# The last rows of a mixture of experts: one-hot products in PSUM in the place of a scatter and a load

## The chip, the core and the metric

The program runs on one core of a Trainium2 chip. The metric is the device time of one execution in microseconds (us). An execution under the profiler is read beside it; its times are counted from the first instruction of the span. The engines are TensorE (PE, with its weight loads as PEld), VectorE (DVE), ScalarE (ACT), GpSimd (POOL) and SyncE (SP, which issues DMAs).

## What is computed

Layer 0 is a non-local convolution block. Layer 1 takes its 2 x 3136 tokens of 256 channels through causal attention and a mixture of eight experts, of which each token uses two:

```python
t = t + attention(ln(t))
xf = ln(t).reshape(-1, 256)
probs = softmax(xf @ gate_w + gate_b)
top2_vals, top2_idx = top_k(probs, 2)
for e in range(8):            # 256 -> 512 -> 256
    y = gelu(xf @ W1[e] + b1[e]) @ W2[e] + b2[e]
    out += cw[:, e, None] * y # cw is 0 but for the two chosen
t = t + out
```

The result is handed back with the channels first, so each tile of 128 tokens has to be transposed at the end.

## The kernel before

**Stages.** Layer 0 and the first projections take about 110 us. Attention runs from there to about 860 us, batch 0 and then batch 1. In the same time each token's two rows (one for each chosen expert) get a place ("slot") in a list sorted by expert, and the normalized rows are scattered into it (`x_slots`, L1302 for both batches). The list has 105 blocks of 128 rows, and a block belongs to one expert. Blocks 0 to 41 hold rows of batch 0 alone, 42 to 56 rows of both, and the later ones rows of batch 1. The first 102 blocks are worked through by `experts` (`MAIN = NBLK - GB = 102`); if the rows need more blocks, or the sums of the softmax are out of bounds, a branch at the end of the program (`tc.If`, L1977) does the rest or does all again. With these inputs it is not entered, so it is a jump to the end. What it compares is `good`, computed by `judge` (L1632, L1633) and loaded into every engine's registers by `count` (L1971) after everything else.

**The expert stage.** From 864 to 1276 us the loop in `experts` takes one block n per step. The order of instructions is written out by hand (`manual_schedule`):

- `fetch` loads a group of three blocks' rows (SP, L1342), `load` works out where the results go (DVE, three small operations, L1367 to L1372: the row number in `y_tokens`).
- `hidden(n)`: 8 products of 128 x 128 x 128 (L1421) and four Gelus on ACT (L1430). In fp32, PE takes each product in two passes, so the profile counts 16.
- `inputs(n + 2)`: two transposes (L1398) and a copy by ACT (L1402).
- `weights(n + 2)`: a copy of the expert's first weights by DVE (L1409).
- `outputs(n - 3)` (`LATE = 3`): 4 products with the expert's second weights (L1440, 8 passes of 256 columns), then the sum with the bias on DVE (L1450, two halves). The block's 128 rows `ys` go, for n below 57, to `y_slots` in slot order, and for n from 42 on POOL scatters them to `y_tokens` in token order (L1457).
- `between()` gives the two `finish` generators a turn, and `experts_of` loads expert numbers into the registers of PE and DVE (L1384).

So second products run three blocks behind first products, and after block 101's first product four second products (98 to 101) are left.

**The finish.** From block 57 on `written` starts `finish(0)` and `finish(1)`. A piece is a pair of tiles of 128 tokens: two sets of rows, one for each of a token's two experts, are brought into SBUF. For batch 0 POOL gathers them from `y_slots` (L1514). For batch 1, whose rows are in token order, SP loads them from `y_tokens` (L1539) once the blocks that can hold them have been scattered (`complete(n)`: the list is sorted, and within an expert by token). DVE adds both, times the gate's weights, to the token's own row (L1554). PE transposes into a bank of PSUM (L1567), ACT copies it out (L1572) and SP stores it (L1573). The tiles `ot` have two buffers, the `y` tiles of batch 1 three. Batch 1's tiles 20 to 24 need block 101 or one close to it, so these pieces come after the last second product. A tile's rows can be loaded only when the scatters that it waits for have landed in DRAM. SP's queue works in order: a store that waits holds up what stands behind it.

Of the kernel before, what the change touches and what calls it, by code (L numbers as in the profile page):

```python
# [10 lines left out]
F32 = mybir.dt.float32  # L11
# [17 lines left out]
def conv_attn_moe_kernel(  # L29
# [74 lines left out]
    XS = C + 2  # L104
# [9 lines left out]
    MAIN = NBLK - GB  # L114
    SCALE = 1.0 / HS**0.5
    LEAST, MOST = 1e-25, 1e25
    assert B == 2 and NBLK % GB == 0 and FULL0 % GB == 0 and QB % (2 * P) == 0 and NS == NB and all(e >= min(N, (i + 1) * W) for i, (_, e) in enumerate(SEGS))
# [318 lines left out]
    wts = [const.tile([P, NCH, 2], F32, name=f"wt{b}") for b in range(B)]  # L436
# [12 lines left out]
    def layer1(nm, general):  # L449

        with ExitStack() as whole:
# [491 lines left out]
            def dispatch(b):  # L943
# [345 lines left out]
                for n in range(NCH):  # L1289
# [9 lines left out]
                    if b:  # L1299
                        nc.vector.tensor_copy(xr[:kk, C:], t[:kk, n, TOKEN : SLOT + 1])  # L1300
# [18 lines left out]
            def experts(w1s, w2s, b2s, ex, es, ps6, between, need, written):  # L1319
# [40 lines left out]
                def load(g, xb, other):  # L1360
# [3 lines left out]
                    if b:  # L1364
# [3 lines left out]
                            eq, xb[:, :, C + 1], sid[:, s - FULL0 : e - FULL0], ALU.is_equal  # L1368
                        )
                        nc.vector.tensor_scalar(eq, eq, -float(N), float(N + OFF), ALU.mult, ALU.add)  # L1370
                        to = ex.tile([P, GB], U32, tag="to", bufs=4, name=f"to_{nm}_{g}")
                        nc.vector.tensor_tensor(to, eq, xb[:, :, C], ALU.add)  # L1372
# [62 lines left out]
                def outputs(n, state):  # L1435
# [20 lines left out]
                    if n >= FULL0:  # L1456
                        s = nc.gpsimd.indirect_dma_start(  # L1457
# [16 lines left out]

                fetched, groups, ids, xin, wb, act = [], [], [], {}, {}, {}
                for n in range(-1, MAIN + LATE):
# [14 lines left out]
                    if 0 <= n - LATE < MAIN:  # L1491
                        outputs(n - LATE, act.pop(n - LATE))
# [5 lines left out]
            def finish(b, oy, bufs):  # L1498
# [27 lines left out]
                def complete(n):  # L1526


                    return min(MAIN, (2 * N + 2 * n * P) // P + E)

# [29 lines left out]
                def store(n, m, k, ys, rows):  # L1560
# [12 lines left out]
                    nc.sync.dma_start(  # L1573
# [5 lines left out]
                parts = deque(pairs())  # L1579
                while b == 0 and (parts or ahead):  # L1580
# [14 lines left out]
                while parts or ahead or added:  # L1595
                    now = worked[0]
                    over = now == MAIN
                    if parts and len(ahead) + bool(added) < bufs:
                        n, m, k = parts[0]
                        of = complete(n + m)  # L1600
                        if over or now >= min(of + GAP, max(of, MAIN - 1)):
                            ahead.append((now, load(*parts.popleft())))
                            yield True
                            continue
                    if added and (over or now > added[0]):
                        store(*added[1])
                        added = None
                        yield True
                    elif ahead and not added and (over or now >= ahead[0][0] + GAP):
# [431 lines left out]
```

## Time and profile before

| | us |
|---|---|
| median of 3 runs | 1336.9 (1336.3 to 1340.93) |
| the profiled execution's own time | 1298.01 |
| its span | 1296.3 |
| PE busy | 1251.2 (97%) |
| DVE, ACT, POOL busy | 792.1, 611.2, 351.1 |
| last second product ends | 1276.0 |
| last scatter issued | 1277.3 |
| last store issued | 1288.0 |

The page of a profile gives busy time by engine and then the span in 40 slices, one digit for each (9 is 90% busy or more); a slice is 32.4 us here. `PEclk` is the clock that TensorE was granted, in tenths. The chain is the work that ended last, followed backwards: at each step to what released it. In its listing by time a row has start, length and what ran. A row of a line has the engine, the operation, the tiles written and read, shape and count.

### The profile page before, as it was taken

How to read it: one execution, taken by the hardware profiler on the slowest of the kernel's cores; microseconds unless marked ns; L12 is line 12 of the kernel's file. 1: busy time of each engine (PE TensorE's matmuls, PEld its weight loads, DVE VectorE, ACT ScalarE, POOL GpSimd, SP SyncE). 2: the span in 40 equal slices, each digit the busy share in tenths (PEclk: the TensorE clock that was granted, in tenths of full speed). 3: DMA queues.
4: the chain of work that ended last, by engine and by line, in shares of the span. 5: the costliest groups of instructions: out<-in, count | busy, mean ns of one | idle time of the engine just before them, and what ended most of it. 6: DMA issues, size and time to landing. Idle time of an engine off the chain costs nothing.

```text
span 1296.3 us, 28049 instructions
## 1 busy us (share of the span) xinstructions
PE 1251.2 (97%) x10569; PEld 821.7 (63%) x10569; DVE 792.1 (61%) x1659; ACT 611.2 (47%) x1228; POOL 351.1 (27%) x317
## 2 busy tenths in 40 slices
PE   8998999999999999999999999999999999999994
PEld 7874445444444454534444444469899899999993
DVE  1582557676777764668687877755675443465553
ACT  0144555565656555356555655552433333444441
POOL 1102412110002204221115760000047312675641
PEclk9999999999999999999999999999999999999997
DMA  9994011000000000100001243231135443576553
GB/s 304 384 310 165 16 25 32 25 9 25 9 17 9 26 1 12 38 9 16 9 9 62 93 158 108 60 111 50 58 123 171 128 114 95 148 234 200 183 162 104
DMA packets 110656, 123.55 MB, mean 95 GB/s; under 512 B 20020, under 2 KB 100261, under 8 KB 110513
## 3 DMA queue, kind: packets, MB, share of 16 engines
q1 hardware_dynamic: 97104, 93.12, 23.7%
q0 software_dynamic: 9984, 25.76, 5.9%
q10 hardware_dynamic: 3424, 2.78, 0.7%
q8 instruction: 87, 1.43, 0.5%
q14 instruction: 57, 0.46, 0.1%
HBM read 62.65 MB, written 60.41 MB: 95 GB/s over the span
## 4 chain that ended last, share of the span: by engine, by line
PE 80%; DVE 6%; issue 5%; DMA 3%; ACT 2%; POOL 2%; POOLq 0%; DVEq 0%; ACTq 0%; SPq 0%
PE yp_f L700 17%; PE sc_f L660 16%; PE ht_f L1421 13%; PE yp_f L1440 12%; PE qk_f L540 6%; PE cp L330 3%; PE v_f L557 3%; DVE acc_f L682 3%; PE gram L261 3%; PE pp_f L610 2%; POOL x_slots L1302 2%; ACT st_f L668 2%; PE tp_f L1398 2%; DMA kept<-t 1%; PE sp_f L724 1%
## 5 line engine op out<-in xcount | busy, mean ns | idle before, releaser
L668 ACT ACTIVATE st_f<-sc_f 128x896 f32<-128x896 f32 (+5 forms) x400 | 331.0, 840 | 214.7 <-PE sc_f L660 197.3
L682 DVE TENSOR_TENSOR acc_f<-acc_f,st_f 128x896 f32<-128x896 f32 (+5 forms) x372 | 379.6, 1020 | 67.3 <-ACT st_f L668 55.8
L700 PE MATMUL yp_f<-st_f,v_f 64*64 64x448 f32 (+6 forms) x3184 | 339.8, 501 | 4.3 <-DVE st_f L670 3.0
L660 PE MATMUL sc_f<-qT_f,kT_f 64*64 64x448 f32 (+6 forms) x3184 | 339.7, 499 | 3.3 <-ACT st_f L668 2.1
L1430 ACT ACTIVATE g_f<-ht_f,b1b 128x128 f32<-128x128 f32 x408 | 116.7, 369 | 222.5 <-PE ht_f L1421 222.5
L660 PEld LDWEIGHTS sc_f<-qT_f,kT_f 64*64 64x64 f32 x3184 | 122.4, 133 | 154.4 <-issue 124.7
L700 PEld LDWEIGHTS yp_f<-st_f,v_f 64*64 64x64 f32 x3184 | 119.8, 133 | 155.3 <-issue 131.1
L1421 PE MATMUL ht_f<-xT_f,w_f 128*128 128x128 f32 x1632 | 200.3, 276 | 0.8 <-ACT xT_f L1402 0.8
L1421 PEld LDWEIGHTS ht_f<-xT_f,w_f 128*128 128x128 f32 x1632 | 197.1, 193 | 5.7 <-ACT xT_f L1402 1.0
L712 POOL TENSOR_TENSOR qT_f<-both_f 128x448 f32<-128x448 f32 x28 | 37.0, 1322 | 488.5 <-ACT both_f L711 488.5
L1302 POOL DMA_INDIRECT x_slots<-xr_f,idx x100 | 111.2, 1112 | 127.4 <-DVE xr_f L1300 90.0
L511 POOL TENSOR_SCALAR xn_f<-t 128x256 f32<-128x256 f32 (+1 forms) x50 | 80.3, 1614 | 170.9 <-PE xp_f L526 66.2
L1409 DVE COPY w_f<-w1s_f 128x1024 f32 x102 | 71.6, 704 | 55.3 <-PE ht_f L1421 53.6
L1457 POOL DMA_INDIRECT y_tokens<-ys_f,to_f x60 | 62.4, 1040 | 120.6 <-DVE ys_f L1450 95.2
L1450 DVE TENSOR_TENSOR ys_f<-yp_f,kT_f 128x128 f32<-128x128 f32 x102 | 29.6, 290 | 100.7 <-PE yp_f L1440 96.5
L540 PE MATMUL qk_f<-px_f,wat 128*128 128x512 f32 (+2 forms) x224 | 88.1, 546 | 1.2 <-ACT px_f L532 1.2
L540 PEld LDWEIGHTS qk_f<-px_f,wat 128*128 128x128 f32 x224 | 40.6, 190 | 46.9 <-issue 41.6
L670 DVE TENSOR_TENSOR st_f<-st_f,keep 128x256 f32<-128x256 f32 (+1 forms) x112 | 45.4, 405 | 32.8 <-ACT st_f L668 32.8
L678 DVE COPY acc_f<-st_f 128x896 f32<-128x896 f32 x28 | 17.7, 633 | 77.1 <-ACT st_f L668 76.8
L1440 PE MATMUL yp_f<-w2s_f,g_f 128*128 x204 | 61.1, 382 | 0.0
L1440 PE MATMUL yp_f<-v_f,g_f 128*128 x204 | 61.1, 381 | 0.0
L1440 PE MATMUL yp_f<-px_f,g_f 128*128 x204 | 60.9, 380 | 0.0
(255 smaller groups left out, 1252.1 us busy)
## 6 DMA issues: line engine op xcount, KB each, us to landing
x_slots<-fill SPq DMA_DIRECT2D x1, 8127.0 KB
xb_f<-x_slots SPq DMA_DIRECT2D x60, 129.0 KB
x_slots<-fill SPq DMA_DIRECT2D x1, 7296.0 KB
y_slots<-ys_f SPq DMA_DIRECT2D x57, 128.0 KB
kept<-t SPq DMA_DIRECT2D x2, 3200.0 KB
x<-in_x_dram SPq DMA_DIRECT2D x14, 448.0 KB
rb_f<-inverses SPq DMA_DIRECT2D x56, 112.0 KB
xr<-in_x_rows_dram SPq DMA_DIRECT2D x12, 512.0 KB
```

Source lines behind the costliest of these rows:

```text
L511: nc.gpsimd.tensor_scalar(xn[:k, a], ts[b][:k, n + a, :C], ts[b][:k, n + a, MEAN : MEAN + 1], ts[b][:k, n + a, RSTD : RSTD + 1], ALU.subtr ...
L540: nc.tensor.matmul(ps[:, :w], wat[:, c, d0 : d0 + P], px[:, s % 2, c, :w], start=(c == 0), stop=(c == NH - 1),)
L660: nc.tensor.matmul(ps[h : h + HS, a, c0:W], kT[hp][rows, j * P + h : j * P + h + HS], qT[rows, hp, q0 + c0 : q0 + W], start=True, stop=True,)
L668: nc.scalar.activation(st[:k, :, c0:], ps[:k, :, c0:W], AF.Exp, scale=SCALE)
L682: nc.vector.tensor_tensor(acc[:k, :, c0:], acc[:k, :, c0:], st[:k, :, c0:], ALU.add)
L700: nc.tensor.matmul(yp[a * HS : (a + 1) * HS, h // HS, c0:W], v[hp][h : h + HS, j, a, :HS], st[h : h + HS, a, c0:], start=first, stop=bool( ...
L1302: s = nc.gpsimd.indirect_dma_start(out=xds[b], out_offset=bass.IndirectOffsetOnAxis(ap=idxs[b][:kk, k, n : n + 1], axis=0), in_=xr[:kk], i ...
L1409: nc.vector.tensor_copy(w, w1s[:, :, bass.ds(e, 1), :].rearrange("p c e h -> p c (e h)"))
L1421: nc.tensor.matmul(ht[:, k, :], w[:, c, k * P : (k + 1) * P], xT[:, c, :], start=(c == 0), stop=(c == NH - 1),)
L1430: nc.scalar.activation(g[:, k, :], ht[:, k, :], AF.Gelu, bias=b1bs[b][:, k, i : i + 1])
L1440: nc.tensor.matmul(yp[:, :C], g[:, k, :], w2s[k][:, bass.ds(e, 1), :].rearrange("p e d -> p (e d)"), start=(k == 0), stop=(k == KH - 1),)
L1457: s = nc.gpsimd.indirect_dma_start(out=y_tokens, out_offset=bass.IndirectOffsetOnAxis(ap=to[:, n % GB : n % GB + 1], axis=0), in_=ys, in_o ...
```

## The change

- The expert loop's second products run one block behind the first ones in the last blocks (`behind`): three behind below block 97, two at 97, one after it. The loop ends one step after the last block.
- The rows of blocks 99 to 101 (`DIRECT = MAIN - GB = 99`) are no longer scattered to `y_tokens`. They stay in SBUF. For each of these blocks DVE makes a matrix of 128 x 448 (`hots`): row p holds the gate's weight of the block's row p in the column of its token, and 0 elsewhere. The column counts from token 2688 (`LAST = 21`, `REST = 448`). The start is an iota on POOL when block 56 is done, compared with the row's token by DVE. `place` multiplies the block's rows (as stationary operand, in two halves of 128 channels) with that matrix and sums in two banks of PSUM, channels first.
- What blocks up to 98 gave to the last 448 tokens is loaded from `y_tokens` by `last_rows` (four loads on SP, after product 98), weighted and added to the token's own row by `add_rows` (DVE), and added into the same banks by products with the identity (`place_rows`). `store_last` copies the banks out, one by ACT, one by DVE, and stores them from ACT's queue.
- The part of `y_tokens` that holds these tokens is filled with zeros early (two DMAs on SP), since not all of it is written now.
- A row of `x_slots` carries two words more, the token's two weights (`XS = C + 4`); to have them in one place the weights of batch 1 are kept in `ts[1]`.
- `finish(1)` ends with tile 20 and starts with a single tile; its last piece (tiles 19 and 20) is added after the last product. Its last store goes through ACT's queue.
- `good` is loaded before the last but one second product (`decide`), not after everything; the remaining pieces are drained (`settle`) ahead of the last store. The branch's other side redoes blocks from 99 on.

The diff, without the branch's other side and renamed columns:

```diff
-    XS = C + 2
+    XS = C + 4
...
+    DIRECT = MAIN - GB
+    def complete(n):
+        return min(MAIN, (2 * N + 2 * n * P) // P + E)
+    LAST = max(n for n in range(NCH) if complete(n) <= DIRECT)
+    REST = N - LAST * P
...
-    wts = [const.tile([P, NCH, 2], F32, name=f"wt{b}") for b in range(B)]
+    wts = [const.tile([P, NCH, 2], F32, name="wt0"), ts[1][:, :, C + E - 2 : C + E]]
...
-                        nc.vector.tensor_copy(xr[:kk, C:], t[:kk, n, TOKEN : SLOT + 1])
+                        nc.vector.tensor_copy(xr[:kk, C:], t[:kk, n, C + E - 2 : SLOT + 1])
...
+                        if s == DIRECT:
+                            one_hots(xb, eq)
+                            return xb, None
...
                     if n >= FULL0:
+                        if n >= DIRECT:
+                            direct[n] = ys
+                            worked[0] = n + 1
+                            return
                         s = nc.gpsimd.indirect_dma_start(
...
+                def one_hots(xb, eq):
+                    w, v = (es.tile([P, GB], F32, tag=f"w{k}", bufs=1, name=f"w{k}_{nm}") for k in range(2))
+                    nc.vector.tensor_tensor(w, eq, xb[:, :, C], ALU.mult)
+                    nc.vector.tensor_scalar(eq, eq, -1.0, 1.0, ALU.mult, ALU.add)
+                    nc.vector.tensor_tensor(v, eq, xb[:, :, C + 1], ALU.mult)
+                    nc.vector.tensor_tensor(w, w, v, ALU.add)
+                    for a in range(GB):
+                        nc.vector.tensor_scalar(
+                            hots[a], hots[a], xb[:, a, C + 2 : C + 3], w[:, a : a + 1],
+                            ALU.is_equal, ALU.mult,
+                        )
+                def last_rows(oy):
+                    pair = y_tokens.rearrange("(a n) d -> a n d", a=2)
+                    def space(c, n):
+                        return oy.tile([P, 2, C], F32, tag=f"y{B - 1}{c}", bufs=3, name=f"y{c}_{nm}_{n}")
+                    def fetch(to, of):
+                        i = nc.sync.dma_start(out=to, in_=of).ins
+                        tc.add_to_no_dep_group(f"y_tokens_{nm}", i)
+                    y = [space(c, LAST) for c in range(2)]
+                    for c in range(2):
+                        fetch(y[c], pair[c, LAST * P : (LAST + 2) * P].rearrange("(n p) d -> p n d", p=P))
+                    for a in range(2):
+                        tail.append((LAST + a, [y[c][:, a] for c in range(2)]))
+                    for n in range(LAST + 2, NCH):
+                        k = chunk(n)
+                        y = space(n % 2, n)
+                        fetch(y[:k], pair[:, n * P : n * P + k].rearrange("a p d -> p a d"))
+                        tail.append((n, [y[:k, c] for c in range(2)]))
+                def add_rows():
+                    b = B - 1
+                    for n, y in tail:
+                        k = chunk(n)
+                        for c in range(2):
+                            nc.vector.scalar_tensor_tensor(
+                                y[0], y[c], wts[b][:k, n, c : c + 1],
+                                y[0] if c else ts[b][:k, n, :C], ALU.mult, ALU.add,
+                            )
+                def place(n):
+                    if not sums_of:
+                        sums_of.extend(
+                            ps6.tile([P, 512], F32, tag="tp", bufs=2, name=f"tail{o}_{nm}") for o in range(NH)
+                        )
+                    for o in range(NH):
+                        nc.tensor.matmul(
+                            sums_of[o][:, :REST], direct[n][:, o * P : (o + 1) * P], hots[n - DIRECT],
+                            start=(n == DIRECT), stop=(n == MAIN - 1),
+                        )
+                def place_rows():
+                    for n, y in tail:
+                        k = chunk(n)
+                        for o in range(NH):
+                            nc.tensor.matmul(
+                                sums_of[o][:, (n - LAST) * P : (n - LAST) * P + k],
+                                y[0][:, o * P : (o + 1) * P], ident[:k, :k], start=False, stop=False,
+                            )
+                def store_last(o):
+                    ot = hots[o]
+                    (nc.vector.tensor_copy if o else nc.scalar.copy)(ot, sums_of[o][:, :REST])
+                    nc.scalar.dma_start(out=out[B - 1, o * P : (o + 1) * P, LAST * P :], in_=ot)
+                def behind(n):
+                    return 3 if n < MAIN - 5 else 2 if n == MAIN - 5 else 1
-                for n in range(-1, MAIN + LATE):
+                for n in range(-1, MAIN + 1):
...
-                    if 0 <= n - LATE < MAIN:
-                        outputs(n - LATE, act.pop(n - LATE))
+                    if n == MAIN - 1:
+                        decide()
+                    for m in sorted(act):
+                        if m > n - behind(n):
+                            break
+                        outputs(m, act.pop(m))
+                        if m == DIRECT - 1:
+                            last_rows(last_pool[0])
+                        if m == MAIN - 2:
+                            add_rows()
+                        if m > DIRECT:
+                            place(m - 1)
+                    if n == MAIN:
+                        place_rows()
+                        place(MAIN - 1)
+                        store_last(0)
+                        settle()
+                        store_last(1)
+                        break
...
+                if b:
+                    parts = deque([(0, 1, P), *pairs(1, LAST)])
...
-                        if over or now >= min(of + GAP, max(of, MAIN - 1)):
+                        if over or now >= min(of + GAP, max(of, DIRECT)):
...
-                        store(*added[1])
+                        store(*added[1], nc.scalar if over else nc.sync)
...
-                    elif ahead and not added and (over or now >= ahead[0][0] + GAP):
+                    elif ahead and not added and (over or sum(ahead[0][1][:2]) < LAST and now >= ahead[0][0] + GAP):
...
+            for c in range(2):
+                nc.sync.dma_start(
+                    out=y_tokens[c * N + LAST * P : (c + 1) * N].rearrange("(n p) d -> p n d", p=P // 2),
+                    in_=fill[: P // 2, :C].unsqueeze(1).to_broadcast([P // 2, REST // (P // 2), C]),
+                )
...
                 def written():
...
+                    for a in range(GB):
+                        hots.append(hot.tile([P, REST], F32, name=f"hot{a}_{nm}"))
+                        nc.gpsimd.iota(
+                            hots[a], pattern=[[1, REST]], base=LAST * P - OFF, channel_multiplier=0,
+                            allow_small_or_imprecise_dtypes=True,
+                        )
...
+                def settle():
+                    while queue:
+                        pull(every=True)
+                def decide():
+                    if not general:
+                        verdict.append(count(1))
```

## The prediction

> **What bounds the kernel now.** I read the page first, then the chain that ended last in order of time, then the stretches of the last 20 us, then the instructions of the branch that closes the program.
>
> ```profile
> span 1296.3 us, 28049 instructions
> PE   8998999999999999999999999999999999999994
> DMA  9994011000000000100001243231135443576553
> ```
>
> TensorE (PE) is full in all slices but the last, so whatever stands beside it in the expert stage is free. Only the last slice has room for a gain. The chain there, after block 101's first product (times from the span's start):
>
> ```profile
> 1267.35 1.79 PE ht_f L1421 x16
> 1269.13 5.20 PE yp_f L1440 x24
> ...
> 1277.34 3.85 DMA y_tokens<-ys_f,to_f
> ...
> 1281.33 2.75 DMA y_f<-y_tokens
> ...
> 1285.48 1.25 PE yo_f L1567 x4
> ...
> 1287.72 0.27 ACT ot_f L1572
> ```
>
> Four second products (98 to 101) drain after the last first product. Then the last rows go to DRAM (3.85) and come back (2.75), are added, transposed, copied and stored. The stretches show that PE also slows down there (columns: busy time and count of PE, PEld, DVE, ACT, POOL; granted clock; DMA share; GB/s):
>
> ```profile
> 1276.00:1278.00 2.00, 0.70 (x5) 0.31 (x3) 1.03 (x4) 0.59 (x1) 0.75 (x2) 1.00 0.07 23
> 1280.00:1282.00 2.00, 0.00 (x0) 0.00 (x0) 0.97 (x3) 0.00 (x0) 0.00 (x0) 0.50 0.25 84
> 1288.00:1290.00 2.00, 0.00 (x0) 0.00 (x0) 0.00 (x0) 0.00 (x0) 0.00 (x0) 0.50 0.63 181
> ```
>
> Nothing computes after 1288, and the span ends at 1296.3. The last 8 us belong to the `good` load (L1971) and the taken branch (L1977); a row's last figures are first and last start:
>
> ```profile
> L1971 ACTq TENSOR_LOAD <-good x1: 757/757/757, 1288.0 to 1288.0; - x1
> L1971 SPq TENSOR_LOAD <-good x1: 551/551/551, 1288.4 to 1288.4; - x1
> ```
>
> ```profile
> L1977 SPq EVENT_SEMAPHORE  x9: 17/17/17, 1292.0 to 1294.6; - x9
> L1977 ACTq EVENT_SEMAPHORE  x2: 17/17/17, 1292.3 to 1292.4; - x2
> L1977 PEldq EVENT_SEMAPHORE  x2: 51/51/51, 1292.5 to 1292.6; - x2
> ...
> L1977 PEldq COMPARE_BRANCH  x1: 4744/4744/4744, 1287.6 to 1287.6; - x1
> L1977 ACTq COMPARE_BRANCH  x1: 50/50/50, 1288.9 to 1288.9; - x1
> L1977 SPq COMPARE_BRANCH  x1: 54/54/54, 1289.1 to 1289.1; - x1
> ```
>
> ACT branches at 1288.9 and goes on at 1292.3 (3.4), SP at 1289.1 and 1292.0 (3.0), PE at 1287.6 and 1292.5 (4.9). SP stalls once more: its two waits there sum to 4.9.
>
> [...]
>
> **The change part by part.** *Start.* SP's queue gets two fills of 448 rows (0.92 MB) behind the `kept` stores. At the 318 GB/s of 80 to 100 us that is 2.9 us. DMA is busy until about 111, and SP issues nothing more until 123.97. Cost 0; without that cover 2.9. The filled slots are 8 bytes a row wider (8127 KB becomes 8190), 0.2 us at the same place. The page's chain has "DMA kept<-t 1%" there, which looks like a critical store. I don't believe it: the ACT row said to wait for it has a 1.28 us table load ending at the same instant (109.28 to 110.57). So 0, at worst 0.2. The 50 wider x_slots scatters (L1302, 1112 ns each) move 0.8% more bytes: 0. The strided weights cost 0. The first y_tokens scatter now waits for the fills, which landed hundreds of us before it: 0.
>
> *Block 56.* Three iotas stand on POOL's queue ahead of the gathers and scatters. `number` took 0.22 us for 105 elements and `rev`, 8 elements, 0.14, so 448 take about 0.52, together 1.6. POOL is busy 10 to 12 us in 20, and nobody waits for a gather at once (two blocks lie between load and sum): 0. Batch 1's pairs now begin at odd tiles; loads, sums, transposes and stores per tile stay as they were: 0.
>
> *Block 96.* The one-hots add to DVE two small operations (0.16 each) and three of 128x448. No row is like these. Nearest are the 128x1024 copy at 0.70 (L1409), giving 0.3 for 448, and the 128x896 sum at 1.02 (L682), giving 0.5. I take 0.5, in all 1.8 us. DVE is busy 12 us in 20 and waits up to 1.7 us for PE before each weight copy; block 98's weights are needed two blocks later. Cost 0; if the cover fails, 1.8.
>
> *One block behind.* In blocks 97 and 98 two second products follow each other. The same instructions run in another order; the Gelu (1.14) that block m's product needs started a whole first product earlier. POOL needs 0.97 for each scatter, less than the 1.73 between two such products. PE stays full, so the order gains nothing by itself. It moves products 98 and 99 ahead of the last first product.
>
> *PE to the end.* Before, product 101's first part ends at 1269.13. Two second products more stand ahead of that point (2 x 1.73) and, by the instruction order, four transposes fewer (82, not 86; 0.44): 1272.15. Then follow: second product 100, 1.73, to 1273.88. Placing 99: a pass of 256 columns costs 1.73/8 = 0.216, so one of 448 0.378, and 2 halves x 2 passes 1.51: 1275.39. Six transposes 0.71: 1276.10. Second product 101: 1277.83. Placing 100: 1279.34. The identity products, 16 passes at 1.79/16 less the half tile, 1.67: 1281.01. Placing 101: 1282.52, its first half at 1281.76. The clock stays at 1.00[...].
>
> *What could stop PE.* Scatter 98 starts about 1267.0 and lands by 1270.8 (3.85); four loads on SP land by 1275.1. DVE adds them (eight at about 0.46) after rows 100, from 1274.75 to 1278.4; rows 101 leave DVE at 1278.9. Placing 101 needs them at 1281.0: 2 us to spare. Three scatters, six loads, their 3.85 + 2.75 and all after them leave the path. What is late next is PE itself.
>
> *Stores.* ACT copies the first half (0.53, from 0.59 for 512) to 1282.5 and issues (0.38). Tile 19's transposes end at 1283.1, copied by 1283.8, issued by 1284.2; the second half, copied by DVE by 1283.3, is issued by 1284.6. Before, the last issue ended at 1288.4: 3.8 earlier.
>
> *End.* The load of `good` stands ahead of second product 100, on all five queues. Its wait is for values ready since 1018 us (L1633), so behind it ACT's and SP's last tiles, DVE's rows 100 and PE's product lose the load alone, and all have slack but PE. On ACT 0.76 and SP 0.55 leave the end, and PE's 0.31 hides in its queue as the block loads (L1384, 0.76) do, beside which PE stayed full; if it doesn't, 0.3. SP's last store leaves about 1281, so both its fetches are over by 1286.3. ACT branches at 1284.65 and, after 3.4 us, is through at 1288.1; PE at 1283.2 + 4.9, also 1288.1. The closing barrier then needs 0.9 to 1.1: 1289.2. The last store lands 2.5 us[...] after 1284.4, and from there SP needs 2.2 (1294.1 to 1296.3): 1289.1. Stores met branch fetches in the trace: packets of the stores still ran at 1291 to 1292, 3 us after their issue. I add 0.8 for that: **1290.0, -6.3 us**. The profiled execution took 1298.01, 1.7 more than its span, which I leave. The median shown is 1336.9, 39 us above; no view says where these lie, so I carry the difference over: **1330.6**.
>
> **Rivals.** *More is gained:* no collision, fetches quicker with fewer engines at once; the end is at 1288.6, -7.7: 1329.2. For it: DVE's branch took only 3.0. Against: PE's took 4.9 in the same trace. *Given back:* three stores of 229 to 262 KB in a row on ACT land 2 us later beside the fetches, and one DVE wait costs 1 us: -3.3, 1333.6. For it: the late packets. *It does nothing:* a fetch or landing that I count as hidden is still last, 1337. Against: the last issue really moves. *Slower:* **a ring of queues.** On SP, tile 19's loads must wait for PE's transposes of tile 17 (1276.1), since they reuse its buffer. Behind them stand the stores of two output tiles, and their landing frees the tiles that ACT needs for two copies queued ahead of the first half's copy. Two loads and two issues (1.6) and 2.5 to land end at 1280.2, the copies at 1281.0, 1.0 us before the first half is ready. Each us over that delays the end. If the hops follow one another and take the scatter's 3.85 three times, 1276.1 + 1.6 + 11.6 + 0.9 is 1290.2, 8.2 late, and the kernel 1.9 us slower: 1338.8. It decides from 7.3 us of delay on. Against: stores landed in about 2.5.
>
> **How the numbers follow.** What this measurement can tell from no change is about 0.5%, 6.7 us, and my estimate lies just inside. As worked out (-7.0 to -5.4): 0.47, a quarter of it beyond 6.7. More gained (-7 to -9.5): 0.25. Given back (-5.4 to -1.5): 0.17. Nothing: 0.04. Slower, by the ring or a stall I don't see: 0.07, of which 0.05 by more than 6.7. Faster 0.37, same 0.58, slower 0.05. The range 1327.5 to 1335.5 takes in the first three, with the 1.8 and 0.2 us of failed cover.
>
> **What would show it.** Right: PE full until about 1282.5, at clock 1.00; no wait of `y_f` for `y_tokens` after 1276; `good` loaded before 1276; last store issued by 1284.6, SP's branch near 1281; span near 1290. Wrong: idle before a `tail` product (DVE late), ACT's first-half copy waiting on a tile's store (the ring), or over 4 us between the last issue and the barrier.

## The result, and the profile after

| | before | after |
|---|---|---|
| median, first set (20 runs each) | 1336.97 (1333.2 to 1341.84) | 1329.8 (1323.74 to 1336.66) |
| ratio, first set | | 0.9945, 95% interval 0.9931 to 0.996 |
| median, later set (25 and 5 runs) | 1297.88 (1294.96 to 1300.44) | 1291.33 (1289.9 to 1291.92) |
| ratio, later set | | 0.9950, 95% interval 0.9937 to 0.9964 |
| profiled spans | 1296.3, again 1296.6 | 1331.9, again 1289.6 |

The change gains 7.2 us in the first set (1336.97 less 1329.8) and 6.5 in the later one; 6.3 was forecast. The two sets lie 39 us apart for both kernels, so a time is only compared within its set. The profiles must be matched in the same way. The first profile of the changed kernel runs at the first set's level and the first profile of before at the later one's. The page of after, whose slices are 33.3 us long, shows some of the places where the long execution lost time:

```profile
span 1331.9 us, 28093 instructions
...
PE   8998999999999999999998999999999899899997
...
PEclk9999999999999999999999999999999899899999
```

The two 8s of the clock are the slices 1032 to 1066 and 1132 to 1166 us; PE's own 8 in the middle is 699 to 733. None of the placing runs in these three. A second profile of the changed kernel, in the later set, has none of these 8s in the clock and takes 1289.6. Against it the loss is spread: block 0 starts 11.4 us later in the long execution, and blocks 0 to 96 take 31.2 us more. So I read all kernels by one length that does not see the body: from the end of the last first product to the end of the span. I call it **the tail**. The order of the change puts 3.0 us of products ahead of that point (two second products, 3.46, less four transposes, 0.44), so a changed kernel's tail plus 3.0 stands against a tail of before. The traces bear this out: from the start of block 96 to that point, before takes 22.61 us and after 25.60.

The chain of after, to be held against the chain of before in the prediction:

```profile
1311.12 1.79 PE ht_f L1433 x16
1312.91 1.73 PE yp_f L1452 x8
1314.64 1.50 PE tail_f L1544 x4
1316.14 0.70 PE yo_f L1675 x6
1316.84 1.92 PE yp_f L1452 x8
1318.77 1.50 PE tail_f L1544 x4
1320.27 1.92 PE tail_f L1554 x16
1322.19 0.96 PE tail_f L1544 x2
...
1323.18 0.54 ACT hot_f L1562
...
1323.74 1.97 DMA out_dram<-hot_f
...
1325.75 0.58 ACT ot_f L1680
```

The scatter (3.85) and the load (2.75) are gone from the chain, and PE works without a gap for 10.2 us after the last first product. But there is one DMA left in it, 1.97 us between two copies of ACT: the copy of tile 19 (with tile 20) waits for a store. I had not priced that.

The clock and the closing branch of after (the columns of the stretches are those of the prediction; the branch's rows have first and last start at the end):

```profile
1320.00:1322.00 2.00, 2.00 (x17) 1.77 (x15) 1.36 (x3) 0.85 (x2) 0.00 (x0) 1.00 0.44 154
1322.00:1324.00 2.00, 2.00 (x9) 1.14 (x9) 0.07 (x1) 0.53 (x1) 0.00 (x0) 1.00 0.59 166
```

```profile
L2109 SPq EVENT_SEMAPHORE  x9: 17/17/17, 1325.1 to 1330.2; - x9
...
L2109 ACTq EVENT_SEMAPHORE  x2: 17/17/17, 1330.6 to 1330.7; - x2
...
L2109 SPq COMPARE_BRANCH  x1: 54/54/54, 1322.4 to 1322.4; - x1
...
L2109 ACTq COMPARE_BRANCH  x1: 50/50/50, 1327.4 to 1327.4; - x1
```

The clock is whole, where before had 0.50. ACT branches at 1327.4 and is through at 1330.6 (3.1); SP's last wait, for the last store, ends at 1330.2; the end is 1331.9.

All profiles in one table. "Issue" is the time from the last first product to the end of the last store's issue, "end" from there to the end of the span; both sum to the tail. Spans are taken to 0.1 us, so the last two hold to 0.05. The ratio is against runs of before on the same chip.

| kernel | issue | end | tail | tail + 3.0 where the order is changed | ratio (95%) |
|---|---|---|---|---|---|
| before, first profile | 19.25 | 7.91 | 27.17 | 27.2 | |
| before again | 19.08 | 7.91 | 26.98 | 27.0 | 0.9998 (0.9989 to 1.0006) |
| before, count early | 18.83 | 7.49 | 26.31 | 26.3 | 0.9990 (0.9984 to 0.9997) |
| before, order | 16.07 | 7.82 | 23.88 | 26.9 | 0.9988 (0.9979 to 0.9996) |
| before, start part | 19.03 | 5.58 | 24.61 | 24.6 | 0.9982 (0.9975 to 0.9988) |
| before, two more issues | 19.12 | 5.89 | 25.00 | 25.0 | 0.9977 (0.9970 to 0.9984) |
| after, first profile | 14.50 | 4.49 | 18.99 | 22.0 | 0.9945 (0.9931 to 0.9960) |
| after again | 15.08 | 4.20 | 19.28 | 22.3 | 0.9950 (0.9937 to 0.9964) |
| after, count late | 13.10 | 5.10 | 18.20 | 21.2 | 0.9945 (0.9931 to 0.9958) |
| after, three behind | 17.49 | 5.53 | 23.02 | 23.0 | 0.9962 (0.9949 to 0.9976) |
| after, third buffer | 13.29 | 5.45 | 18.74 | 21.7 | 0.9953 (0.9939 to 0.9966) |
| after, no identity products | 15.21 | 4.09 | 19.29 | 22.3 | 0.9952 (0.9939 to 0.9966) |
| after, no branch | 12.98 | 2.88 | 15.86 | 18.9 | 0.9938 (0.9922 to 0.9953) |
| after, tile 19 first | 12.42 | 5.17 | 17.59 | 20.6 | 0.9940 (0.9926 to 0.9955) |

### The profile page after: what moved, and what is told of

The parts are those of the page before. It is cut to its first block, busy times and chain, and to the rows that moved or that the text cites. A ratio compares the mean times of both kernels' runs of the same rounds, so it can differ in the third digit from the quotient of the medians.

```text
span 1331.9 us, 28093 instructions
## 1 busy us (share of the span) xinstructions
PE 1276.9 (96%) x10589; PEld 832.4 (62%) x10589; DVE 794.3 (60%) x1665; ACT 608.7 (46%) x1227; POOL 347.9 (26%) x317
## 3 DMA queue, kind: packets, MB, share of 16 engines
q8 instruction: 87, 1.43, 0.5%
## 4 chain that ended last, share of the span: by engine, by line
PE 87%; DVE 6%; issue 3%; ACT 3%; DMA 2%; DVEq 0%; ACTq 0%; SPq 0%
PE yp_f L709 19%; PE sc_f L669 18%; PE ht_f L1433 14%; PE yp_f L1452 13%; PE qk_f L549 6%; PE v_f L566 3%; PE cp L339 3%; PE gram L270 3%; DVE acc_f L691 2%; PE pp_f L619 2%; PE tp_f L1410 2%; ACT st_f L677 2%; PE sp_f L733 1%; DMA y_tokens<-fill 1%; PE yo_f L1675 1%
## 5 line engine op out<-in xcount | busy, mean ns | idle before, releaser
L1433 PE MATMUL ht_f<-xT_f,w_f 128*128 128x128 f32 x1632 | 207.2, 279 | 9.0 <-issue 8.0
L1433 PEld LDWEIGHTS ht_f<-xT_f,w_f 128*128 128x128 f32 x1632 | 201.0, 195 | 15.7 <-issue 10.3
L1473 POOL DMA_INDIRECT y_tokens<-ys_f,to_f x57 | 57.6, 1011 | 131.9 <-DVE ys_f L1462 108.9
```

Source lines behind the costliest of these rows:

```text
L1433: nc.tensor.matmul(ht[:, k, :], w[:, c, k * P : (k + 1) * P], xT[:, c, :], start=(c == 0), stop=(c == NH - 1),)
L1473: s = nc.gpsimd.indirect_dma_start(out=y_tokens, out_offset=bass.IndirectOffsetOnAxis(ap=to[:, n % GB : n % GB + 1], axis=0), in_=ys, in_o ...
```

## The experiments

**Before again.** The kernel before, unchanged.

> The kernel before, unchanged, for a second profile. Theory A (the 40 us that the profiled execution of the changed kernel loses ahead of the last first product belong to executions, not to the change): the span can lie anywhere from 1296 to 1340, lost in steps at places with no relation to the change; the stretch after the last first product is again 27.2 (within 0.7). Rival (the change slows the body, and the kernel before always runs its body as in its first profile): a span within 3 us of 1296 again.

The span was 1296.6 and the tail 26.98. That is theory A's tail, but the span is also the rival's: a second profile of before did run its body as the first. So this run alone did not settle whether the change slows the body; the next one did.

**The changed kernel again.** Unchanged.

> The changed kernel, unchanged, for a second profile beside the kernel before on one chip. Theory A (the change gains 6 to 7 us, all after the last first product, whatever the body costs in that execution): the body within 1 us of the kernel before, the stretch after the last first product 18.2 to 19.3 us against 27.0 to 27.2, and the whole 6 to 7.5 us faster. Rival (the body of the changed kernel is slower, as its first profile seemed to say): the last first product ends 5 us or more later than in the kernel before, beyond the 3.0 of the order.

6.5 us faster, tail 19.28. Its last first product ends at 1270.32, 0.7 us after that of before again (1269.62), although 3.0 us of products were moved ahead of it: the body is not slower. The 39 us go with the set of runs. Of the 2.3 us that it is even ahead at the start of block 96, 0.4 had gone by block 0 and 0.2 from there to block 35; 1.1 lie at one stall of PE by block 41, where the rows of batch 1 come first, and 0.6 behind that (see "Blocks 56 and 96" below). From blocks 35 to 43 the thirteen profiles of the later level took 32.5 to 34.9 us, with a gap of 2.1 to 3.0 before a transpose. Two stretches behind that gap, of before and of after again:

```profile
1030.00:1032.00 2.00, 2.00 (x7) 1.59 (x7) 0.73 (x2) 0.03 (x1) 0.00 (x0) 0.58 0.90 258
1032.00:1034.00 2.00, 2.00 (x12) 2.00 (x11) 0.49 (x2) 0.00 (x0) 0.00 (x0) 0.57 0.40 134
```

```profile
1030.00:1032.00 2.00, 1.74 (x9) 1.61 (x10) 1.78 (x5) 0.37 (x1) 0.00 (x0) 1.00 0.85 237
1032.00:1034.00 2.00, 2.00 (x18) 1.95 (x17) 0.49 (x2) 0.00 (x0) 0.00 (x0) 1.00 0.73 245
```

The mean clock is 0.58 and 0.57 in the first (it stood at 0.50 from 1030.3 to 1033.7) and 1.00 in the second, where 18 products fit in place of 12. In four of the thirteen profiles it stayed whole: after again, no identity products, tile 19 first, and before with the order alone. These are the four shortest stretches (32.5 to 33.4 us; the others 34.2 to 34.9). That is three of seven profiles of changed kernels and one of six of before; no line of the placing runs there, and the numbers are too small to say that the change has a part in it. Between 0.8 and 2.4 us of any comparison of two profiles hang on it, so only the tails are compared below.

**The count early.** In the kernel before, the load of `good` moves to where the change has it, right behind block 101's first product. (In this order second product 98 follows it, not 99, as the expectation says.)

```diff
+                    if n == MAIN - 1 and not general:
+                        verdict.append(count(1))
                     if 0 <= n - LATE < MAIN:
                         outputs(n - LATE, act.pop(n - LATE))
...
-    n_done = count(1)
+    n_done = verdict[0]
```

> The kernel before, with one thing of the change: the load of the count that decides the closing branch stands ahead of second product 99's place in the order, not at the end. Theory A (the rows' way through DRAM was the cost; the early count is worth its own load on SP or ACT, if that): 0 to -0.8 us against the kernel before, and 26.4 to 27.2 us from the end of the last first product to the end of the span, where the kernel before had 27.17. Theory B (most of the gain is the end of the program: count and branches taken early): -3 us or more, the same stretch 24 us or less.

The tail fell by 0.7 to 0.9, the time by 1.3 us (0.001 of 1298.2; interval 0.4 to 2.1). That is a little more than theory A allowed (a tail from 26.4 on, 0.8 us at most) and far from theory B.

**The count late.** The changed kernel, with that load put back to the end.

```diff
-                    if n == MAIN - 1:
-                        decide()
...
-    n_done = verdict[0]
+    n_done = count(1)
```

> The changed kernel, with the load of the count put back to the end. Against the changed kernel, whose stretch from the end of the last first product to the end of the span was 18.99 us: theory A +0.5 to +1.8 us (the load on ACT, 0.76, and SP's branch no longer early), stretch 19.5 to 20.8. Theory B (the early count brings most of the gain): +4 us or more, stretch 23 or more, and no gain left against the kernel before.

Neither. The tail was 18.20, shorter than with the early count (18.99 and 19.28). At the end ACT did load for 0.84 us, and its end part grew from 4.2 or 4.5 to 5.1. But the last issue came 1.4 to 2.0 us sooner, because tile 19's copy did not wait for a store. The early count gives no gain here; the wait is taken up below.

**The order alone.** In the kernel before, second products one block behind as in the change; scatters and loads kept.

```diff
-                    if 0 <= n - LATE < MAIN:
-                        outputs(n - LATE, act.pop(n - LATE))
+                    for m in sorted(act):
+                        if m > n - behind(n):
+                            break
+                        outputs(m, act.pop(m))
```

> The kernel before, with only the order of the change: second products one block behind in the last blocks, scatters and loads kept. Theory A (TensorE is full up to the last product, so order alone gains nothing): within 0.7 us of the kernel before; the stretch after the last first product is shorter by the 3.0 us of products that now stand ahead of it, 23.7 to 24.7 us, and that much longer before it. Theory C (a shorter drain is itself the gain): -4 us or more, the stretch 20 us or less.

Tail 23.88, in the window that theory A gave: 26.9 with the 3.0. (From block 96 to the last first product this kernel took 26.06 us, 3.4 more than before, so 27.3 is the fairer sum. Either way the tail gains nothing.) The time is 1.6 us better by the ratio (interval 0.5 to 2.7), more than A's 0.7, but the span was 1296.5 against 1296.6 of before again, with the clock whole behind the stall at block 41. Theory C's 4 us are not there.

**Three behind.** The changed kernel with the old order: `behind` gives 3 throughout.

```diff
-                    return 3 if n < MAIN - 5 else 2 if n == MAIN - 5 else 1
+                    return LATE
```

> The changed kernel with second products three blocks behind to the end, as before the change; rows still placed by one-hot products. The loads of the last rows then start after product 98, which comes after the last first product. Theory A (the order serves to hide scatter 98 and the loads): TensorE waits 3 to 4 us ahead of the identity products, and the stretch after the last first product is 22.0 + 4.5 = 26.5 us (25 to 29, the upper end if the clock halves in the wait); +3 to +7 us against the changed kernel. Rival (the order is idle, the placing alone is the gain): no wait, stretch 22.0, within 1 us of the changed kernel.

Theory A was wrong here. The tail was 23.02, 0.7 to 1.0 more than the changed kernel's with its 3.0 (1.8 more than with the count late, where tile 19's copy does not wait for a store, as it doesn't here), and PE did not wait for the last rows. DVE adds them (columns: start, length, what, and in brackets the idle time before it and what ended it) while PE is at the identity products, which take them tile by tile:

```profile
1273.15 2.12 SPq L1512 DMA_DIRECT2D y_f<-y_tokens  x4
...
1275.89 0.48 DVE L1532 SCALAR_TENSOR_TENSOR y_f<-y_f,t 128x256 f32<-128x256 f32 x1 [0.77 <-DMA y_f<-y_tokens]
...
1278.51 1.90 DVE L1532 SCALAR_TENSOR_TENSOR y_f<-y_f,t 128x256 f32<-128x256 f32 x4 [0.44 <-DMA y_f<-y_tokens]
1279.16 2.09 PE L1554 MATMUL tail_f<-ident,y_f 128*128 128x128 f32 x16
```

I had let the first identity product wait for the last row, and had taken 3.85 us for a scatter that let the loads go after 2.4 (POOL began at 1270.71). Its time is 0.9962 of before, the changed kernel's 0.9950: the intervals overlap. So by the tails the order is worth 0.7 to 1.8 us in the new scheme; by time that is not shown.

**The start part alone.** The kernel before with wider slots, strided weights and the two fills.

```diff
-    XS = C + 2
+    XS = C + 4
...
+            for c in range(2):
+                nc.sync.dma_start(
+                    out=y_tokens[(c + 1) * N - 448 : (c + 1) * N].rearrange("(n p) d -> p n d", p=P // 2),
+                    in_=fill[: P // 2, :C].unsqueeze(1).to_broadcast([P // 2, 448 // (P // 2), C]),
+                )
```

> The kernel before, with only the start of the change: slots two elements wider, weights kept beside the scores with a stride, two fills of 448 rows of y_tokens. Theory A: 0, within 0.5 us; the stretch after the last first product stays at 27.2, and the start up to 130 us within 0.3 us of the kernel before. Rival (what the profile shows as lost in the middle of the changed kernel is the price of these parts): slower by 5 us or more.

Both theories were wrong: it was 2.3 us **faster** (0.0018 of 1298.2), and the tail shows it (24.61): behind the last issue the end took 5.58 us, not 7.91. SP's waits from 1288 on (total, times, longest), in before again and in this kernel:

```profile
SPq L1977 <- SPq L1977: 4.9, 2, 2.7
```

```profile
SPq L1982 <- SPq L1982: 2.5, 1, 2.5
```

SP stalls twice after its branch in before, here once. In before again the second stall was from 1292.24 to 1294.40, ahead of a wait for a transfer that had landed at 1286.63: not the wait itself was late.

**Two more issues.** Is it the data or the length of SP's program? The kernel before with two stores of 128 rows at the start and nothing else.

```diff
+            for c in range(2):
+                nc.sync.dma_start(out=y_tokens[(c + 1) * N - P : (c + 1) * N], in_=fill[:P, :C])
```

> The kernel before, with two stores of 128 rows of y_tokens at the start and nothing else: two instructions more on SP, no wider slots, no strided weights. The kernel with the start part alone was 2.4 us faster than before, against the forecast, and its SP passed its closing waits without the stall of 2.0 to 2.2 us that the kernel before shows between two of them. Theory D (that stall is a second fetch of instructions, and where it falls depends on the length of SP's program): the stall is away here too, stretch after the last first product 24.5 to 25.3. Rival (the wider rows, the strided weights or the fill of the rows bring the 2.4): the stall stays, stretch 26.7 to 27.3.

Theory D held: tail 25.00, time 0.9977 (3.0 us), one stall. SP's waits again, then the packets of queue q14 that fetched instructions (number, MB, share) at the end, in this kernel from 1287 us on and in before again from 1288 on:

```profile
SPq L1979 <- SPq L1979: 2.9, 1, 2.9
```

```profile
q14 instruction: 7, 0.06, 2.7%
```

```profile
q14 instruction: 8, 0.07, 2.5%
```

Two instructions more on SP, one fetch less at the end, and 2 us less. (In the whole program the count is no use: before has 57 in its first profile and 56 again. From 1265 us on, the four profiles with the stall have 10 such packets and the two without it 9.) The other queue that fetches instructions, q8, has 87 packets of 16384 bytes in before (1.43 MB); those of q14 are half as large (0.47 MB in 57). In the first profile of before SP stands from 1289.1 to 1292.0 and from 1292.2 to 1294.1; one packet of q8 and four of q14 start in the first stretch, one and two in the second. That SP, and any engine behind its branch, stands for such fetches is my reading of these times. The second stall took 1.9 to 2.2 us in the four profiles without added stores (before twice, count early, order). That it goes with the two issues is shown. No run added instructions without stores, so that it is the length alone is not.

**The wait of tile 19.** Two kernels. In the first, tile 19 gets a buffer that is free by then:

```diff
-                    ot = oy.tile([P, NH, 2 * P], F32, tag="ot", bufs=2, name=f"ot_{nm}{b}_{n}")
+                    ot = oy.tile([P, NH, 2 * P], F32, tag="res" if via is nc.scalar else "ot", bufs=3 if via is nc.scalar else 2, name=f"ot_{nm}{b}_{n}")
```

> The changed kernel, with the output tile of the last two stores of whole tiles in buffers of its own (those of the residual rows, no longer used there), so that tile 19's copy on ACT does not wait for tile 17's store to land. Theory A (that wait, 1.8 us, stands on the chain that ends last): the copy of tile 19 follows the first half's copy and issue at once, the last store is issued 1.3 to 1.8 us earlier after the last first product, and the stretch is 17.2 to 17.7 us, not 18.99. Rival (the end is set by the branch fetches or by when stores land beside them, whatever the issue): the stretch stays within 0.4 of 18.99.

In the second, `place_rows()` is left out, so what came by way of `y_tokens` is missing in the last 448 columns:

```diff
-                        place_rows()
                         place(MAIN - 1)
```

> The changed kernel without the identity products: the rows that came by way of y_tokens are loaded and added, and not placed into the sums (left out of the output's last 448 columns). They took 1.92 us of TensorE. If TensorE alone sets the end: stretch after the last first product shorter by 1.9, 17.1 us. If the wait of tile 19's copy for tile 17's store sets it (theory A): the first half's copy comes 1.9 earlier, tile 19's copy does not, the second half's store is still behind it, and the stretch is shorter by 0 to 0.5.

The wait is real: with its own buffer the last issue came at 13.29, not 14.50 or 15.08; without the identity products the first half's copy ran earlier and the last issue not at all (15.21). ACT's rows in the second kernel:

```profile
1278.77 0.54 ACT L1562 COPY hot_f<-tail_f 128x448 f32<-128x448 f32 x1
1279.34 0.36 ACTq L1563 DMA_DIRECT2D out_dram<-hot_f  x1
1282.93 0.59 ACT L1679 COPY ot_f<-yo_f 128x512 f32<-128x512 f32 x1 [3.62 <-DMA out_dram<-ot_f]
```

ACT stood for 3.62 us before tile 19's copy and, as the name says, for a store of another `ot` tile: the same buffer, tile 17's store. So 1.92 us of PE less moved nothing: behind the first half's copy it is this wait, not PE, that sets the last issue. But the third buffer moved the end by 0.25 to 0.5 only (18.74), not by theory A's 1.3 to 1.8: the part after the last issue grew to 5.45. ACT's branch took 3.5 us there, 2.9 in after again, and the last store's last piece landed 3.6 us after its issue, not 2.3.

**No branch.** The changed kernel without `tc.If` and what lies under it.

```diff
-                    if n == MAIN - 1:
-                        decide()
...
-    n_done = verdict[0]
-    with tc.If(n_done < P):
...
-        late()
```

> The changed kernel without the closing branch and what lies under it (the redone layer for tokens that the fast path can't take, and the late blocks; with these inputs neither runs). Theory A (after the change the end is set by ACT's branch, 2.8 to 3.5 us, and by a part of the last store that lands late behind the fetches): the last store lands within 2.3 us of its issue, and the stretch after the last first product is 15.5 to 17 us. Rival (landing and the closing barrier set it anyway): within 0.7 us of the changed kernel.

The last store had landed 1.9 us after its issue and the tail was 15.86: 2.3 to 3.4 us shorter than with the branch, as theory A said. By time it is 0.9938, which the intervals don't separate from the changed kernel. Tile 19's copy had no store to wait for either; ACT's rows in after again and here:

```profile
1281.15 0.36 ACTq L1563 DMA_DIRECT2D out_dram<-hot_f  x1
1283.41 0.58 ACT L1680 COPY ot_f<-yo_f 128x512 f32<-128x512 f32 x1 [2.29 <-DMA out_dram<-hot_f]
```

```profile
1283.37 0.36 ACTq L1563 DMA_DIRECT2D out_dram<-hot_f  x1
1284.00 0.58 ACT L1678 COPY ot_f<-yo_f 128x512 f32<-128x512 f32 x1 [0.66 <-PE yo_f L1673]
```

In after again the row names the first half's store as the releaser; the semaphore that ACT waits on is that of tile 17's store. Fifteen of its sixteen pieces landed from 1281.28 to 1281.48 and the last at 1283.05. A fetch of instructions (one packet on q8, 0.88 us) started at 1280.98. In the first profile of after it was the same: fifteen pieces by 1323.62, the last at 1325.40, a fetch on q8 from 1322.48 on (1.46 us). So it was in all five profiles of changed kernels with the early count and the new order: the last piece came 3.8 to 4.0 us after the start of the issue. Without a branch, all sixteen landed within 0.22 us.

I take this fetch for PE's, by its time. It starts 0.9 to 1.9 us after PE's branch in every profile with a branch, and ahead of SP's branch in three (with tile 19 first at 1279.71, where SP branches at 1280.35). With the count late, PE branched 0.4 us later behind that store (0.55 after the start of its issue, not 0.17), and tile 17's pieces landed within 0.2 us. That the fetch holds the piece up is read from these times; no run moved the fetch alone.

**Tile 19 first.** A version meant to use this: tile 19 in its own buffer, its transposes ahead of the last placing, its store on SP.

```diff
                         place_rows()
+                        settle()
                         place(MAIN - 1)
                         store_last(0)
-                        settle()
                         store_last(1)
...
-                    via.dma_start(
+                    nc.sync.dma_start(
```

> The changed kernel, with tile 19 in a buffer of its own, its transposes ahead of the last placing and its store on SP, so that ACT's last two issues are the halves. Theory A (from the last issue on the end is one fetch and one landing long): the last issue comes 12.4 to 12.8 us after the last first product (13.3 with the buffer alone), stretch 17.6 to 18.4. Rival (a floor that the issue doesn't move): 18.7 or more.

Last issue at 12.42, tail 17.59: both as forecast, 1.4 to 1.7 us shorter than the changed kernel's. Its median of 1289.37 against 1291.33 points the same way; the ratios' intervals overlap (0.9926 to 0.9955 and 0.9937 to 0.9964), so that it is faster than the changed kernel is not shown by time.

## Why the prediction was right, and where it wasn't

The sign and the size held: 6.3 us forecast, 7.2 and 6.5 measured. The mechanism held up to the first half's copy: the way through DRAM is gone and PE is the chain. Behind that copy it failed: a wait for a store, not PE, sets the last issue. That the number came so close is in part luck: the tails gained 1.1 to 1.6 us less than the 6.3, and the medians 1.3 to 2.5 us more than the tails.

- **What bounds it.** Right in the main. Most of what the change gains can be read in the tail, from 27.0 or 27.2 to 22.3 or 22.0 with the 3.0: 4.7 to 5.2 us. The rest of the 6.5 to 7.2 is not seen in the tails. In the pair of profiles of the later set (1296.6 and 1289.6, 7.0 apart) 2.3 us lie ahead of block 96, 1.1 of them at the stall by block 41; the intervals of the times reach down to 4.7 (0.9964 of 1297.9).
- **Start: cost 0.** Right that nothing is paid. Wrong as a step: it puts two DMAs more into SP's program, and the second of the two stalls (4.9 us in sum) that I put down as hidden by an early branch goes with two such issues alone, for 2.0 to 2.4 us of tail.
- **Blocks 56 and 96: 0.** No run separates them, and nothing is paid; something is even gained. From block 43 to 96 six of the seven profiles of changed kernels at the later level took 205.0 us (count late 205.5), the six of before 205.6 to 206.3. Two transposes fewer stand there (66, not 68), and in five of the six PE waits 0.2 to 0.6 us ahead of a transpose at block 69. The prediction left transposes as they were.
- **One block behind: nothing by itself.** Right (26.9 or 27.3). The moved 3.02 was measured as 2.99. In the new scheme the order has a use, which the prediction did not price.
- **PE to the end.** Right up to the first half's sum: no gap, clock 1.00. Tile 19's four transposes behind it took 0.60 in after, at 1.00; in before, at 0.50, the last two sets of four took 1.30 and 1.25. The term was low: from the last first product to the first half's sum I had 9.61 us, the chain shows 10.25. Product 101 took 1.92, not 1.73; the identity products 1.92, not 1.67; the last half placing 0.96, not 0.75. These three make 0.65. For the rows' way, the prediction's 3.85 for a scatter did not carry over: with three behind, the loads went 2.4 after POOL began. Of the last five scatters of before the trace has the landing of two, 3.5 and 2.3 us after their start.
- **Stores.** Failed step: "Tile 19's transposes end at 1283.1, copied by 1283.8". SP did stand before its stores in before, 36.4 us in eight waits for ACT's copies from 1225 on, 10.5 the longest. I had checked the ring of queues against the first half's copy, where it had 1.0 us to spare, and not against the next copy, which reuses the buffer of tile 17. That copy began 13.1 or 12.8 us after the last first product, not 11.0 (1283.1 less 1272.15), so the last issue was 2.1 to 2.6 late against 12.45. In its place stands a wait until 1283.1 in after again, 12.8 us after the last first product, for the one late piece of tile 17's store. The rival that would have made the kernel slower was there, at another place, and stayed far below its 7.3 us.
- **End.** I had 5.4 us behind the last issue, with 0.8 for stores meeting fetches. It took 4.49 and 4.20: the other engines' branches were over by the time ACT came. The 2.5 for the last store to land was my estimate. In before seven of the last twelve stores landed 1.7 to 2.5 us after the start of their issue, five 3.4 to 4.9, the last two (4.6 and 4.2) among these; the last of the first profile of after took 3.3. Where the last issue comes earlier and a branch follows, it takes 5.1 to 5.5. So of the 1.2 to 1.8 us by which a third buffer brings the last issue forward, 1.0 to 1.3 are lost again behind it, and the forecast tail of 17.85 (1290.0 less 1272.15) missed by 1.1 to 1.4 only.
- **`good` early: 0.76 on ACT.** It is worth 0.7 to 0.9 of tail in the kernel before. In the changed one it gains nothing: with the count late the tail is 0.8 to 1.1 us shorter. My reading is that the earlier branch brings a fetch into tile 17's store.
- **Carried to the median.** Right: the gain is 0.55% and 0.50% at levels 39 us apart.

Which part brought how much can't be summed: start part 2.3, count 1.3 and order 1.6 by the ratios make 5.2, but the first two act on the same stalls at the end as the rest. Against a kernel before without SP's second stall (start part 24.6, two more issues 25.0) the changed kernel's tail, with its 3.0, is only 2.3 to 3.0 us shorter. Nearly half of the gain in the tail could thus be had by two more issues, without any placing. What stays open is why the medians improve by 1.3 to 2.5 us more than the tails (6.5 to 7.2 against 4.7 to 5.2), of which 0.6 to 1.3 may be the stretch of blocks 43 to 96, and whether the clock behind the stall at block 41 has to do with it.

## What to carry to other kernels

When a chain ends in DRAM and the engine that would replace the round trip is idle behind it, even 7 us of added work on that engine can pay (here 6.96 for the placings and the identity products, in after again, and a tail 4.7 to 5.2 shorter). Then look at every copy behind it, not only the one on the chain: a reused buffer made tile 19's wait 2.0 and 2.3 us for a store (both profiles of after). In the last 10 us, count instruction fetches as traffic: with the early count a fetch ran beside tile 17's store, and one piece landed 1.6 to 1.8 us behind the others; with the count late all landed within 0.2. And before a gain of 2 us at the end is put down to a change, see whether a few more instructions alone bring it: two more issues took 2.0 to 2.2 off the tail.

## What was not expected of the hardware

- Two more DMA issues on one queue took a stall of 1.9 to 2.2 us off the end of the program, some 3 us behind a taken branch.
- A store of 256 KB lands in sixteen pieces; with a packet of instructions fetched at the same time (0.9 to 1.5 us), one piece came 1.6 to 1.8 us after the other fifteen (both profiles of after), and ACT, which waited for the store, waited for that one (2.0 and 2.3 us).
- ACT's branch took 2.8 to 3.1 us with the other engines' branches over (both profiles of after, no identity products) and 3.9 us beside three others (tile 19 first).
- After a gap of 2.2 us in PE's products its clock fell to 0.50 for 3.4 us in before; after a longer one at the same place, 2.95 us, it did not in after again. So the gap's length alone did not decide it; what did is not shown.
